# A two-layer graph attention kernel: row factors, attention columns and one transpose of the first two graphs on TensorE, their work interleaved

## The chip, the cores and the metric

The kernel runs on one core of a Trainium2 chip. The metric is the device time of the whole launch in microseconds (us). Engines are called PE (TensorE), DVE (VectorE), ACT (ScalarE), POOL (GpSimd) and SP (SyncE, which only issues DMAs here). PE has a clock that can be granted in full or in part; the profile calls it PEclk.

## What is computed

64 graphs of 256 nodes with 512 features in float32 go through two layers. Cut to what matters:

```python
# layer 0: 8 heads of 64 units
feats   = einsum('bnf,hfu->bhnu', X, W)
e_self  = einsum('bhnu,hu->bhn', feats, a_self)
e_neigh = einsum('bhnu,hu->bhn', feats, a_neigh)
dense   = leaky_relu(e_self[..., :, None] + e_neigh[..., None, :], 0.2)
att     = softmax(dense + -1e10 * (1 - A[:, None]), -1)
x = layernorm(x + relu(einsum('bhij,bhju->bhiu', att, feats) + b))
# layer 1: 8 heads of 64, q, k, v from W_qkv
attn = 0.33 * softmax(q k^T / 8) + 0.33 * adj + 0.33 * exp(-adj)
x = layernorm(x + (attn v) W_out + b_out)
```

`e_self` and `e_neigh` are linear in X, so the kernel computes them as two more columns per head of the weights of layer 0: W times a_self and W times a_neigh (the "attention columns", U and U + 1 of `wf`). The exponential of the leaky sum is split into a factor for each row (`grow`, for every head a row of 256 values and the maximum of the neighbour term), which all 128 partitions need, and a factor for each column (`ccol`); `pT` is the larger of row factor and column factor, times the mask `at`.

## The kernel before

A graph has 2 tiles (T) of 128 nodes and 4 blocks (C) of 128 features. Its work is cut into stages: `proj0` (features of layer 0), `attend0`, `proj1` (q, k and v), `softmax1` and `attend1`. Each stage is a set of steps, and a list written by hand gives their order: `start` for what comes before the loop, `attention0_beside_projections1(b)` and `attention1_beside_projections0(b)` for each graph, and `end`. `do(stage, graph, step)` emits a step, and `in_order` ties every engine to the order of the source. The loop is a pipeline over graphs: in pass b, layer 0's attention of graph b runs beside the q, k, v of graph b - 1, the softmax of b - 1, the output of b - 2 and the features of b + 1.

The products with wf, wqk and wv take seven products of half blocks in place of eight (`seven`, L281): they need sums of the left side (`xC`, `hC`, made by `left_factors`) and of the weights (`right_factors`, L220, and `combine`, L251). Products are named p1 to p7. "qk p1" is the first product of q and k of a graph, the rows `pq_p<-hT` of the profile.

What the change touches, for the first graphs:

- The attention columns. DVE multiplies each of 8 pieces of W with a_self and a_neigh, copied to every partition (`a_bc`), and adds up (L211, L216).
- The features of graph 0 (`features`, L469) use plain W and the transposed rows of x (`xT_rows`); those of graph 1 are seven products (`pf_p`).
- The row factors (`rows`, L419): four transposes (`pr`), a maximum, an exponential and a clamp of 8 rows; then `gs` goes to DRAM and comes back to all partitions as `gb` (1028 KB). `columns` (L441) needs the maximum out of it, `weights` (L517) the rows.
- The output of layer 0 of each graph (`X1`) goes to DRAM as rows (`hs`) and comes back in blocks of 32 (`hb`, L635); DVE transposes the blocks into `hT` (L639), the input of `proj1`.
- `norm0`, `end`, `squares` and `norm` are the layer norm of both tiles of a graph at once: sums on DVE, squares on ACT, three small steps on POOL (L350 to L354), the scaling on ACT (L358).
- The weights of layer 1 are loaded after `start`, and `combine` runs after the first list of graph 0.

PSUM has two pools: "mm" with 4 banks and "sc" with 2 buffers of two banks.

Of the kernel before, what the change touches and what calls it, by code (L numbers as in the profile page):

```python
# [8 lines left out]
FT = mybir.dt.float32  # L9
# [8 lines left out]
def kernel(  # L18
# [29 lines left out]
    nc = tc.nc  # L48
# [99 lines left out]
    a_bc = io.tile([P, 2, H, U], FT, tag="x1", name="a_bc", bufs=3)  # L148
    for k, a in enumerate((a_self, a_neigh)):
        nc.sync.dma_start(  # L150
            a_bc[:, k].rearrange("p h u -> p (h u)"),
            a.rearrange("h u -> (h u)").partition_broadcast(P),
        )
    for c in range(C):
        for g in range(2):
            nc.sync.dma_start(
                wf[c // C2][g][:, c % C2, :, :U],
                w0[g * HG : (g + 1) * HG, c * P : (c + 1) * P, :].rearrange("h p u -> p h u"),
            )
        if c == 1:  # L160
            load_rows(0)
# [45 lines left out]
    for c in range(C):  # L207
        for g in range(2):
            w = wf[c // C2][g][:, c % C2]
            prod = work.tile([P, 2, HG, U], FT, tag="pT", name=f"wa_{c}_{g}", bufs=4)  # L210
            nc.vector.tensor_mul(  # L211
                prod,
                w[:, :, :U].unsqueeze(1).to_broadcast([P, 2, HG, U]),
                a_bc[:, :, g * HG : (g + 1) * HG, :],
            )
            nc.vector.tensor_reduce(  # L216
                w[:, :, U:].rearrange("p h s -> p s h"), prod, AX.X, ALU.add
            )

# [8 lines left out]
    def load_weights1():  # L228

        wk1 = work.tile([P, C2, F], FT, tag="p", name="wk1", bufs=4)  # L230
        wv12 = work.tile([P, C2, F2], FT, tag="both", name="wv12", bufs=4)
        parts = w_qkv.rearrange("(k c p) (h s u) -> s k c p h u", k=2, p=P, s=3, u=U)

        def get(dst, s, k, heads=slice(0, H)):
            for c in range(C2):
                nc.sync.dma_start(
                    dst[:, c].rearrange("p (h u) -> p h u", u=U), parts[s, k, c][:, heads]
                )

        get(wqk_sb[:, 0], 0, 0)  # L240
        get(wqk_sb[:, 1], 0, 1)
        get(wk1, 1, 0)
        get(wqk_sb[:, 6], 1, 1)
        get(wv_sb[:, 0], 2, 0, slice(0, HG))
        get(wv12, 2, 0, slice(HG, H))
        get(wv_sb[:, 1], 2, 1, slice(0, HG))
        get(wv_sb[:, 2], 2, 1, slice(HG, H))
        nc.sync.dma_start(bo_bc, b_out.partition_broadcast(P))
        nc.sync.dma_start(wo_sb, w_out.rearrange("(c p) f -> p c f", p=P))

        def combine():  # L251
            q1, q2, s1, s2, s3, s4, k2 = (wqk_sb[:, i] for i in range(7))
            nc.vector.tensor_add(s1, wk1, k2)
            nc.vector.tensor_sub(s2, s1, q1)
            nc.vector.tensor_sub(s3, q1, wk1)
            nc.vector.tensor_sub(s4, q2, s2)
            right_factors(wv_sb, wv12)

        return combine
# [67 lines left out]
    class LayerNorm:  # L327
# [9 lines left out]
        def mean(self):  # L337
            nc.gpsimd.tensor_scalar_mul(self.nmean, self.sums, -1.0 / F)  # L338

        def squares(self):  # L340
            for t in range(T):
                junk = small.tile([P, F], BF, tag="junk", name="junk", bufs=1)
                nc.scalar.activation(  # L343
                    junk,
                    self.src[:, t, :],
                    AF.Square,
                    bias=self.nmean[:, t : t + 1],
                    accum_out=self.rstd[:, t : t + 1],
                )
            nc.gpsimd.tensor_scalar(  # L350
                self.rstd, self.rstd, 1.0 / F, EPS, op0=ALU.mult, op1=ALU.add
            )
            nc.gpsimd.tensor_tensor(self.rstd, self.rstd, mhalf, op=ALU.pow)
            nc.gpsimd.tensor_mul(self.shift, self.nmean, self.rstd)  # L354

        def apply(self):
            for t in range(T):
                nc.scalar.activation(  # L358
                    self.src[:, t, :],
                    self.src[:, t, :],  # L360
                    AF.Identity,
                    bias=self.shift[:, t : t + 1],
                    scale=self.rstd[:, t : t + 1],
                )


    V0, GB, CCOL, AT, CT = {}, {}, {}, {}, {}

    def proj0(b):
        xT = work.tile([P, C, N], FT, tag="xT", name=f"xT_{b}")  # L370
        xC = work.tile([P, 4, C2, P], FT, tag="xC", name=f"xC_{b}", bufs=1)

        V0[b] = work.tile([P, T, H, UX], FT, tag="v0", name=f"v0_{b}", bufs=1)
        GB[b] = work.tile([P, H, N + 1], FT, tag="gb", name=f"gb_{b}", bufs=1)
# [44 lines left out]
        def rows():  # L419
            pr = ps_tile([H, 2, N], f"pr_{b}")  # L420
            for s in range(2):
# [15 lines left out]
                GB[b].rearrange("p h n -> p (h n)"),  # L437
                gs.rearrange("h n -> (h n)").partition_broadcast(P),
            )

        def columns():  # L441
            nd = small.tile([P, T, H], FT, tag="nd", name=f"nd_{b}", bufs=2)
            nc.vector.tensor_sub(
                nd,
                V0[b][:, :, :, U + 1],
                GB[b][:, :, N].unsqueeze(1).to_broadcast([P, T, H]),
            )
            nc.scalar.activation(CCOL[b], nd, AF.Exp, scale=0.8)  # L448
            nc.scalar.activation(V0[b][:, :, :, U], nd, AF.Exp, scale=0.2)

        def halves(t, g):
            return V0[b][:, t, g * HG : (g + 1) * HG]

        product, add = seven_rows(
            f"pf_{b}",
            xT,
            xC,
            wf_sb,
            [P, HG, UX],
            {10 * (t + 1) + g + 1: halves(t, g) for t in range(T) for g in range(2)},  # L460
        )
# [7 lines left out]
        def features(t):  # L469

            for g in range(2):
                pf = ps_tile([P, HG, UX], f"pf_{b}_{t}_{g}")
                for c in range(C):
                    matmul(
                        pf,
                        xT[:, c, t * P : (t + 1) * P],
                        wf[c // C2][g][:, c % C2],
                        start=(c == 0),
                        stop=(c == C - 1),
                    )  # L480
                nc.vector.tensor_add(halves(t, g), pf, b0_bc[:, g * HG : (g + 1) * HG])
# [10 lines left out]
        def transposes():  # L492
            transpose_blocks(xT, XB[b])
            left_factors(xC, xT)

        return dict(
            xT=transposes,
# [16 lines left out]
    def attend0(b):  # L514
        pT = {}

        def weights(h):  # L517
            pT[h] = work.tile([P, T, N], FT, tag="pT", name=f"pT_{b}_{h}", bufs=4)
            for j in range(T):
                nc.vector.scalar_tensor_tensor(  # L520
                    pT[h][:, j, :],
                    GB[b][:, h, :N],
# [37 lines left out]
        def end():  # L560
            ln = NORM["l0", b] = LayerNorm(X1[b], b, "l0")
            for t in range(T):
# [9 lines left out]
            ln.mean()  # L572
            X.pop(b)
# [6 lines left out]
            squares=lambda: NORM["l0", b].squares(),  # L580
            norm=lambda: NORM.pop(("l0", b)).apply(),
# [5 lines left out]
    def proj1(b):  # L587
# [4 lines left out]
        hb = io.tile([P, C, N // B, B], FT, tag="hb", name=f"hb_{b}", bufs=1)  # L592
        hs = dram.tile([N, F], FT, tag="hs", name=f"hs_{b}")
# [45 lines left out]
        def transposes():  # L639
            transpose_blocks(hT, hb)  # L640
            left_factors(hC, hT)

        return dict(
            blocks=rows_to_blocks,
# [220 lines left out]
    def start():  # L865
        do("proj0", 0, "xT_rows")
        for t in range(T):
            do("proj0", 0, "features", t)
        do("proj0", 0, "rows")
        do("proj0", 0, "aT")  # L870
        do("proj0", 0, "far")
        do("proj0", 0, "shared")
        do("proj0", 0, "columns")
        for h in range(H):
            do("proj0", 0, "scaled", h)

    def attention0_beside_projections1(b):


        do("attend1", b - 3, "squares")  # L880
        do("proj1", b - 1, "qk", "p1")
        do("proj1", b - 1, "qk", "p2")
        if b > 0:
            do("proj0", b, "columns")
        do("proj1", b - 1, "qk", "p6")
        for h in range(HG):
            if b > 0:
                do("proj0", b, "scaled", h)
            do("attend0", b, "weights", h)
        do("attend1", b - 3, "store")  # L890
        do("proj1", b - 1, "qk_add", 11)
        do("proj1", b - 1, "qk", "p5")
        do("proj1", b - 1, "qk", "p7")
        do("attend1", b - 2, "residual")
        do("proj1", b - 1, "qk_add", 22)
        do("attend0", b, "product", 0, 0)
        if b > 0:
            for h in range(HG, H):
                do("proj0", b, "scaled", h)
        do("proj1", b - 1, "qk", "p4")  # L900
# [6 lines left out]
        do("proj1", b - 1, "qk", "p3")  # L907
        do("proj1", b - 1, "qk_add", 12)
        do("proj0", b + 1, "xT")
        if b + 2 < NB:  # L910
            load(b + 2)
# [115 lines left out]
    in_order()  # L1027
    start()
    if NB > 1:
        load(1)  # L1030
        load_adj(1)
    right_factors(wf_sb, wf12)
    combine_weights1 = load_weights1()
    in_order()
    for b in range(NB):
        attention0_beside_projections1(b)
        if b == 0:
            combine_weights1()
            in_order()
# [50 lines left out]
```

The softmax here doesn't subtract the row's maximum and nothing guards it: scores larger than these inputs give would overflow.

## Time and profile before

| | |
|---|---|
| Median of 3 runs | 3186.19 us (3185.43 to 3191.53) |
| Span of the profiled run | 3185.4 us, mean clock of PE 0.990 |
| PE busy | 3116.4 us, 98% |
| DVE busy | 2647.0 us, 83% |
| ACT busy | 1485.6 us, 47% |
| The chain that ended last | PE 85%, DVE 8%, DMA 4% |
| qk p1 of graph 0, 1, 2, 3 starts | 74.57, 118.61, 169.76, 218.37 us |

How to read it: an engine row gives the time in which the engine worked, its share of the span and the number of its instructions. A busy PE isn't yet a PE at its peak, since its matmuls are pipelined. In the time lines a row gives the start, the length, the engine, the line of the source, the operation with output and inputs, the shape and the count, and in brackets the idle time before it with what ended it. Each float32 matmul of the source is two rows of the trace; a transpose is one.

### The profile page before, as it was taken

The numbers are of one execution on the slowest core, as the hardware profiler recorded it, in microseconds if no ns is written. First come the engines' busy times: TensorE is split into PE (matmuls) and PEld (weight loads), VectorE is DVE, ScalarE is ACT, GpSimd is POOL, SyncE is SP. The second block draws the span as 40 slices with busy tenths as digits, with TensorE's granted clock in tenths as the row PEclk, the third lists the DMA queues.
The fourth block names the chain that finished last, engine by engine and source line by source line (L and its number), as shares of the span: only waits on it lengthen the run. The fifth ranks groups of instructions, "written<-read, shape, count | busy, mean of one in ns | idle before, by whom it ended". The sixth has DMA issues, their size and how long they took to land.

```text
span 3185.4 us, 56122 instructions
## 1 busy us (share of the span) xinstructions
PE 3116.4 (98%) x21262; PEld 2502.0 (79%) x21262; DVE 2647.0 (83%) x5152; ACT 1485.6 (47%) x3585; POOL 176.2 (6%) x518
## 2 busy tenths in 40 slices
PE   5999999999999999999999999999999999999997
PEld 4887877877878878878878778778788788788784
DVE  6788888888888888888888888888888888888885
ACT  1444444454454454444444444544544544454442
POOL 0000000000000000000000000000000000000000
PEclk7999999999999999999999999999999999999998
DMA  7344344344343443443443443443443434434421
GB/s 157 76 113 108 98 114 97 102 121 94 104 115 93 112 106 97 111 106 98 114 104 100 115 95 104 121 94 104 121 94 104 115 94 109 105 99 112 108 81 53
DMA packets 764394, 331.88 MB, mean 104 GB/s; under 512 B 696672, under 2 KB 697440, under 8 KB 747744
## 3 DMA queue, kind: packets, MB, share of 16 engines
q1 hardware_dynamic: 764128, 328.30, 40.9%
q8 instruction: 171, 2.80, 0.4%
q14 instruction: 95, 0.78, 0.1%
HBM read 259.80 MB, written 68.16 MB: 103 GB/s over the span
## 4 chain that ended last, share of the span: by engine, by line
PE 85%; DVE 8%; DMA 4%; SPq 1%; issue 1%; ACT 1%; POOL 0%; ACTq 0%; DVEq 0%; POOLq 0%
PE pq_p L292 21%; PE po L828 13%; PE av L539 12%; PE pf_p L292 11%; PE pv_p L292 11%; PE pz L668 7%; PE av L767 7%; DVE pT L520 2%; PE pd L697 2%; DMA gb<-gs 2%; DVE p L757 1%; DVE p L750 1%; PE pr L82 1%; DMA rb<-rs 1%; DVE qk L304 0%
## 5 line engine op out<-in xcount | busy, mean ns | idle before, releaser
L539 PEld LDWEIGHTS av<-v,pT 128*128 128x128 f32 x4096 | 493.9, 194 | 19.0 <-ACT v L485 12.5
L539 PE MATMUL av<-v,pT 128*128 128x65 f32 x4096 | 491.7, 274 | 12.2 <-ACT v L485 12.2
L292 PE MATMUL pq_p<-hC,wqk_sb 128*128 128x128 f32 x4096 | 482.4, 276 | 2.6 <-ACT qk L301 2.6
L292 PEld LDWEIGHTS pq_p<-hC,wqk_sb 128*128 128x128 f32 x4096 | 467.8, 192 | 3.2 <-ACT qk L301 3.2
L828 PE MATMUL po<-wo_sb,oT 128*128 128x512 f32 x1008 | 459.5, 599 | 0.0
L520 DVE SCALAR_TENSOR_TENSOR pT<-gb,ccol,at 128x256 f32<-128x256 f32 x1024 | 416.9, 479 | 24.6 <-ACT ccol L448 17.8
L301 ACT COPY v<-pv_p 128x256 f32<-128x256 f32 x256 | 95.6, 373 | 669.9 <-PE pv_p L292 669.9
L292 PE MATMUL pq_p<-hT,wqk_sb 128*128 128x128 f32 x3072 | 376.0, 279 | 4.8 <-DVE hT L121 4.8
L292 PEld LDWEIGHTS pq_p<-hT,wqk_sb 128*128 128x128 f32 x3072 | 355.2, 193 | 31.3 <-DVE hC L270 24.3
L828 PEld LDWEIGHTS po<-wo_sb,oT 128*128 128x128 f32 x1008 | 181.6, 190 | 204.0 <-issue 202.7
L677 ACT ACTIVATE p<-pz,hide 128x512 f32<-128x512 f32 x512 | 310.3, 689 | 59.3 <-PE pz L668 59.3
L757 DVE TENSOR_TENSOR p<-p,ct 128x1024 f32<-128x1024 f32 x256 | 313.5, 1225 | 8.8
L750 DVE TENSOR_TENSOR p<-p,rb 128x1024 f32<-128x1024 f32 x256 | 309.2, 1208 | 9.2 <-DMA rb<-rs 9.0
L343 ACT ACTIVATE junk<-x,nmean_l 128x512 bf16<-128x512 f32 x256 | 185.0, 723 | 263.7 <-POOL nmean_l L338 259.5
L292 PE MATMUL pv_p<-wv_sb,hC 128*128 128x256 f32 x1024 | 260.5, 387 | 4.8 <-DVE v L304 4.5
L689 DVE SCALAR_TENSOR_TENSOR both<-p 128x512 f32<-128x512 f32 x256 | 176.6, 691 | 98.7 <-ACT p L677 98.5
L485 ACT ACTIVATE v<-v 128x64 f32<-128x64 f32 x1024 | 258.5, 339 | 0.0
L292 PE MATMUL pf_p<-wf_sb,xC 128*128 128x264 f32 x1008 | 256.7, 388 | 0.5 <-ACT v L301 0.5
L668 PE MATMUL pz<-qk 64*128 64x256 f32 x2048 | 256.2, 389 | 0.9 <-ACT p L677 0.8
L767 PE MATMUL av<-p,v 128*64 128x256 f32 x2016 | 245.6, 385 | 0.9 <-DVE p L757 0.9
L668 PEld LDWEIGHTS pz<-qk 64*128 64x128 f32 x2048 | 187.1, 186 | 67.9 <-ACT p L677 26.0
L292 PEld LDWEIGHTS pf_p<-wf_sb,xC 128*128 128x128 f32 x1008 | 191.9, 191 | 33.4 <-ACT v L301 1.3
(107 smaller groups left out, 3693.1 us busy)
## 6 DMA issues: line engine op xcount, KB each, us to landing
gb<-gs SPq DMA_DIRECT2D x64, 1028.0 KB
rb<-rs SPq DMA_DIRECT2D x64, 1024.0 KB, 4.7
x<-in_x_dram SPq DMA_DIRECT2D x64, 512.0 KB
hs<-x SPq DMA_DIRECT2D x64, 512.0 KB
hb<-hs SPq DMA_DIRECT2D x256, 128.0 KB, 3.5
out_dram<-x SPq DMA_DIRECT2D x64, 512.0 KB, 3.0
xb<-in_x_dram SPq DMA_DIRECT2D x252, 128.0 KB, 3.7
adj<-in_adj_dram SPq DMA_DIRECT2D x256, 64.0 KB, 4.5
```

Of the source, the lines that this page charges most:

```text
L292: matmul(d, lhsT, rhs, start=(p in FIRST and i == 0), stop=(i == len(todo) - 1), skip_group_check=True,)
L343: nc.scalar.activation(junk, self.src[:, t, :], AF.Square, bias=self.nmean[:, t : t + 1], accum_out=self.rstd[:, t : t + 1],)
L485: nc.scalar.activation(V0[b][:, t, h, :U], V0[b][:, t, h, :U], AF.Copy, scale=V0[b][:, t, h, U : U + 1],)
L520: nc.vector.scalar_tensor_tensor(pT[h][:, j, :], GB[b][:, h, :N], CCOL[b][:, j, h : h + 1], AT[b][:, j, :], op0=ALU.max, op1=ALU.mult,)
L539: matmul(av[:, k, :], pT[h][:, j, t * P : (t + 1) * P], V0[b][:, j, h, :UA], start=(j == 0), stop=(j == T - 1),)
L668: matmul(pz[:, r, j, :], QK[b][rows, g, 1, j * P : (j + 1) * P], QK[b][rows, g, 0, :], start=True, stop=True,)
L677: nc.scalar.activation(p[:, :, j, :], pz[:, :, j, :], AF.Exp, bias=hide[:, j, b : b + 1], scale=U**-0.5,)
L689: nc.vector.scalar_tensor_tensor(both[g], p[:, :, 0, :], TINY, p[:, :, 1, :], op0=ALU.add, op1=ALU.add)
L750: nc.vector.tensor_mul(p, p, REC[b][:, k : k + 2, g // 2, :] .unsqueeze(2) .to_broadcast([P, 2, T, N]),)
L757: nc.vector.tensor_add(p, p, CT[b].unsqueeze(1).to_broadcast([P, 2, T, N]))
L767: matmul(av[0][r * U : (r + 1) * U, g % 2, :], V1[b][:, j, 2 * g + r, :], PROBS[b][g][:, r, j, :], start=(j == 0), stop=(j == T - 1),)
L828: matmul(po, oT[:, c, t * P : (t + 1) * P], wo_sb[:, c, :], start=(c == 0), stop=(c == C - 1),)
```

## The change

The first two graphs (0 and 1) get an order and some steps of their own; from graph 2 on the steps are those of before. For graphs 0 and 1:

- The attention columns are made by PE: W's blocks are transposed by a product with the identity (`pw`, 64 columns for each head), copied by ACT (`wT`) and multiplied with `a2`, which holds a_self and a_neigh of a pair of heads as columns (`pwa`). DVE copies the few results into wf.
- The row factors stay on the chip: PE spreads each of the 8 rows over all partitions by a product with a selector of ones (`pg`), and DVE's `weights` reads them in PSUM; the maximum is spread by a product with a diagonal.
- Graph 1's features use plain weights too, so that wf's right factors can wait until graph 2.
- Graph 0's output is transposed by PE (`ph`) and not sent through DRAM; its layer norm runs by tiles.
- `start` holds all of graph 0's layer 0 and, between its steps, graph 1's features and row factors and graph 0's q and k; the loop starts with b = 1. The weights of layer 1 are loaded at the start, their combinations are spread over the list in four parts, and w0 is loaded by ACT's queue.

It is for keeping PE at work before the pipeline has filled. The core of the diff:

```diff
+    for g in range(2):
+        for c in range(C):
+            nc.scalar.dma_start(
...
+    a2 = consts.tile([P, HG, 2, 2], FT, name="a2")
+    nc.vector.memset(a2, 0.0)
+    for k, a in enumerate((a_self, a_neigh)):
+        for r in range(2):
+            nc.sync.dma_start(
+                a2[r * U : (r + 1) * U, :, r, k],
+                a.rearrange("(g r) u -> r u g", r=2)[r],
+            )
...
-            nc.vector.tensor_mul(
-                prod,
-                w[:, :, :U].unsqueeze(1).to_broadcast([P, 2, HG, U]),
-                a_bc[:, :, g * HG : (g + 1) * HG, :],
-            )
-            nc.vector.tensor_reduce(
-                w[:, :, U:].rearrange("p h s -> p s h"), prod, AX.X, ALU.add
-            )
...
+    def attention_vectors():
+
+        pwa = ps_tile([P, HG, C, 4], "pwa")
+        for g in range(HG):
+            pw = psum.tile([P, C, P], FT, tag="sc", name=f"pw_{g}", bufs=2)
+            for c in range(C):
+                for r in range(2):
+                    matmul(
+                        pw[r * U : (r + 1) * U, c, :],
+                        wf[c // C2][g // 2][:, c % C2, 2 * (g % 2) + r, :U],
+                        ident,
+                        start=True,
+                        stop=True,
+                    )
+            wT = work.tile([P, C, P], FT, tag="pT", name=f"wT_{g}", bufs=4)
+            nc.scalar.copy(wT, pw)
+            for c in range(C):
+                matmul(pwa[:, g, c, :], wT[:, c, :], a2[:, g], start=True, stop=True)
...
+        def maxima():
...
+            diag = small.tile([H, H], FT, tag="diag", name=f"diag_{b}", bufs=1)
+            nc.vector.tensor_scalar_mul(diag, ident[:H, :H], grow[:, N : N + 1])
+            matmul(pr[:, 1, :H], SEL[0][:, H, :], diag, start=True, stop=True)
...
+        def factors():
...
+            for g in range(2):
+                pg = psum.tile([P, HG, N], FT, tag="sc", name=f"pg_{b}_{g}", bufs=2)
+                for k in range(HG):
+                    matmul(
+                        pg[:, k, :],
+                        SEL[0][:, g * HG + k, :],
+                        grow[:, :N],
+                        start=True,
+                        stop=True,
+                    )
...
+        def from_rows(t):
...
+            for c in range(C):
+                transpose(PT[0][:, t, c, :], X1[b][:, t, c * P : (c + 1) * P])
+            nc.scalar.copy(hT[:, :, t * P : (t + 1) * P], PT[0][:, t])
...
     def start():
...
+        attention_vectors()
+        in_order()
+        for g in range(2):
+            for t in range(T):
+                do("proj0", 0, "features", t, g)
+                do("proj0", 0, "copied", t, g)
...
+        do("proj0", 0, "maxima")
+        do("proj0", 0, "columns")
+        do("proj0", 0, "factors")
+        do("proj0", 1, "xT")
...
+        do("attend0", 0, "end", tiles[0])
+        do("attend0", 0, "squares", tiles[0])
+        do("attend0", 0, "norm0", 0, 1)
+        do("attend0", 0, "norm0", 1, 1)
+        do("attend0", 0, "end", tiles[1])
+        do("attend0", 0, "squares", tiles[1])
+        do("attend0", 0, "norm", tiles[0])
+        do("proj1", 0, "from_rows", 0)
+        do("attend0", 0, "norm", tiles[1])
...
+        combine_weights1(0)
+        do("proj1", 0, "qk", "p1")
+        do("proj1", 0, "from_rows", 1)
+        do("proj1", 0, "hC")
+        do("proj1", 0, "qk", "p2")
+        do("proj1", 0, "qk", "p6")
+        do("proj1", 0, "qk_add", 11)
...
-    for b in range(NB):
+    for b in range(1, NB):
         attention0_beside_projections1(b)
```

What `start` leaves out above, in order: weights and scaling of heads 0 to 3, features of graph 1's first tile, products of these heads, the same for heads 4 to 7 and the second tile, `norm0` of the first tile; and after the add of q: copies of graph 1's second tile, `combine` 1, `shared` of graph 0, adjacency and `far` of graph 1, qk p5 and p7, `maxima`, `columns` and `factors` of graph 1, `combine` 2 and an add.

In the first pass of the loop (b = 1) the steps come in this order: weights of heads 0 to 3, qk p4 and p3, products, weights of heads 4 to 7, `norm0` of the first half, `shared` of graph 1, the right factors of wv and then of wf, xT of graph 2, the values of graph 0, and the features of graph 2.

## The prediction

> **What bounds the kernel now.** I read the page first, then the busy time in stretches, then the time lines of TensorE (PE), VectorE (DVE) and ScalarE (ACT) over the first 125 us.
>
> ```profile
> PE 3116.4 (98%) x21262; PEld 2502.0 (79%) x21262; DVE 2647.0 (83%) x5152; ACT 1485.6 (47%) x3585; POOL 176.2 (6%) x518
> ...
> PEclk7999999999999999999999999999999999999998
> ```
>
> ```profile
> 0.00:118.61 118.61, 76.33 (x426) 65.50 (x426) 74.84 (x161) 34.16 (x87) 3.33 (x14) 0.81 0.59 127
> 118.61:169.76 51.15, 48.77 (x332) 38.88 (x332) 41.74 (x83) 20.36 (x50) 1.82 (x4) 1.00 0.39 93
> 169.76:218.37 48.61, 48.51 (x336) 38.81 (x332) 41.01 (x81) 23.20 (x56) 2.88 (x8) 1.00 0.41 107
> ```
>
> The columns are stretch, length, busy time of PE, weight loads, DVE, ACT, POOL, then the clock. From 169.8 us on PE is never idle and a graph takes 48.6 us. The change touches nothing there: only what runs before qk p1 of graph 1, which starts at 118.61 us. So the question is when that point comes. Before it PE is idle for 42 us and its clock averages 0.81. The time line says where:
>
> ```profile
> 35.88 13.89 PE L539 MATMUL av<-v,pT 128*128 128x65 f32 x64 [12.21 <-ACT v L485]
> ...
> 70.86 1.01 PE L82 MATMUL pr<-ident,v 128*8 128x128 f32 x4 [11.51 <-DVE v L465]
> 74.57 6.07 PE L292 MATMUL pq_p<-hT,wqk_sb 128*128 128x128 f32 x32 [2.70 <-DVE hT L121]
> ...
> 118.61 3.84 PE L292 MATMUL pq_p<-hT,wqk_sb 128*128 128x128 f32 x32 [2.13 <-DVE hT L121]
> ...
> 127.71 2.05 PE L292 MATMUL pq_p<-hC,wqk_sb 128*128 128x128 f32 x16 [1.69 <-ACT qk L301]
> ```
>
> ```profile
> 32.56 0.18 DVE L443 TENSOR_TENSOR nd<-v,gb 128x16 f32<-128x16 f32 x1 [3.35 <-DMA gb<-gs]
> ...
> 81.80 3.26 DVE L520 SCALAR_TENSOR_TENSOR pT<-gb,ccol,at 128x256 f32<-128x256 f32 x8 [0.28 <-ACT ccol L448]
> ```
>
> ```profile
> 107.04 1.52 ACT L358 ACTIVATE x<-x,shift_l,rstd_l 128x512 f32<-128x512 f32 x2 [0.30 <-POOL shift_l L354]
> ```
>
> A line is start, length, engine, line and tiles, and in brackets the idle time before it and what ended it. The reader sees three holes of PE (12.2, 11.5 and 2.7 us), the round trip of the row factors through DRAM in front of the first, and the chain of graph 1: weights pT at 81.80, norm done at 107.04 + 1.52 = 108.56, then rows to DRAM and back, hT, and 118.61.
>
> The clock needs its own look, in stretches of 3.41 us:
>
> ```profile
> 48.57:51.98 3.41, 3.07 (x10) 2.11 (x9) 2.10 (x7) 0.25 (x1) 0.00 (x0) 0.50 0.84 191
> 51.98:55.39 3.41, 3.23 (x7) 2.53 (x8) 0.24 (x2) 1.19 (x4) 0.22 (x1) 0.50 0.68 168
> 55.39:58.81 3.42, 3.42 (x17) 2.92 (x16) 1.49 (x3) 2.39 (x6) 1.10 (x3) 1.00 0.82 297
> 58.81:62.22 3.41, 0.54 (x3) 0.12 (x1) 2.80 (x4) 2.05 (x5) 0.00 (x0) 1.00 0.98 164
> ```
>
> The 64 av of the 35.88 line ran without a pause for 14 us and stayed at half clock (0.50 in every stretch to 51.98); the 264-wide pf_p filled one stretch and the next ran at 1.00; a stretch with 0.54 us of work lost it again.
>
> **What the Trainium skill says.** "TensorE: Matmul & The Clock Gate", Part 1, "What's actually happening": half rate by default, full rate after a busy window of about 3.4 us, windows that run freely. The trace agrees (changes near 28.1, 55.4, 62.2 and 79.3 us, whole windows apart) and adds that narrow work doesn't count as busy: an av takes 217 ns at half clock for 65 columns, a 128-wide pq_p 230. Same page, "LDWEIGHTS (loading the stationary operand)": the load goes by columns. The trace has 190 ns for 128 columns, 137 for 64. Same page, Part 3, "The mechanism": tiles in different places of the array run together. The trace agrees: 16 av of layer 1, 64 columns to each half, take 1.88 us (117 ns each), where full-width pv_p of the same 256 take 216. "DMA: Bandwidth & Descriptors", "Rules for kernel authors": a last dimension that isn't contiguous costs a descriptor per element. That concerns a2 (1024 floats); no run here shows it.
>
> **The change, part by part**, on the clock of the run. Steps come from the rows named; a hand-over between engines costs 0.05 to 0.2 us in the trace.
>
> *Start.* Rows of x come first now, w0 on ACT's queue. Before, 16 KB, 1 MB and x had landed at 10.18. About 1 MB is ahead of the second half of x and the first four w0 blocks: with 0.2 MB by 4 us and 0.77 by 6 us (98 and 283 GB/s), some 7 us. ACT's table load (1.28) now stands behind its eight DMA issues, and the seventh waits for a2. So the first wT copy is done near 11.2 (10.4 to 12.5).
>
> *Attention columns on PE.* Removed: eight pairs of DVE operations (1.32 us each, 7.2 to 17.8). Added: four groups, strictly one after another in PE's order. A group is 8 source matmuls, 16 instructions, to 64 columns (16 x 125 ns = 2.0 us at half clock, 1.0 at full), a wait for ACT's copy (0.16 + 0.59 + 0.06 = 0.81), and 8 instructions against a2, bound by weight loads like av (8 x 217 = 1.74, or 8 x 108 = 0.87). That is 4.55 us at half clock, 2.7 at full. Dense share: 2.0 of 4.55, 44%, less than the av that never woke the clock. I take half clock: 11.2 + 1.74 + 3 x 4.55 = 26.6 us.
>
> *Features of graph 0.* 32 instructions: about 5.1 us at half clock until a full window has passed (11.5 at 445 ns), the rest at 222 ns: 9.7 us, to 36.3. Before: 22.6. This part loses 13.7 us.
>
> *Row factors.* Removed: clamp, gs and gb (25.2 to 32.5) and the right factors of wf ahead of pT (2.6 us). Now: copy 0.45, four transposes 0.6, reduce 0.41, nb 0.14, exp 0.47, the diagonal product, which by the built order waits for exp (0.25), nd 0.18, clamp 0.28, with hand-overs to 39.55; then 8 pg of 216 ns (1.73) and pT, whose first instruction waits for the whole pg tile: 41.4. Before: 35.26. Half of the loss is regained.
>
> *Both graphs.* PE from 39.55: 16 pg 3.5, 32 features of graph 1 7.1, 64 av at full clock 6.9: to 57.1 without a hole; scaled (16 x 246 ns) and pT (2 x 3.3) are hidden beside it. Before, av and pf_p of graph 1 ended at 59.35.
>
> *Norm and hT of graph 0.* Removed: hs and hb by DRAM, DVE's hT, and the queue of combinations on DVE (59.7 to 69.5) before them. Now the last av ends at 55.3 and everything is a chain: norm0 0.65, end 0.75, mean 0.25, squares 0.95, three POOL steps 1.2, the second mean behind them, second squares 0.9, since ACT holds both squares ahead of the first norm, norm 0.8, four transposes 0.5, copy 0.65: qk p1 at 62.5 (before 74.57). PE is idle from 57.1 to 61.25, so its clock falls: p1 3.7 us, and hT's second half is copied only behind it, at 67.9.
>
> *DVE from there.* It sat idle for it; then hC 1.55, add 0.69 (p2 ends 69.3), two copies 0.86, s3 1.22, shared 2.6, adjacency 0.7: 75.6. ACT's far and at (1.6) and copy (0.6) stand before exp (0.5), then diagonal, nd, clamp, pg: 81.1; pT of graph 1 at 81.2. Before: 81.80. The 12 us won at p1 are gone again.
>
> *Graph 1 to the junction.* pT 3.3 and 3.3 with 2.8 for the wait on p3 and its add, norm0 1.2, shared 2.65, and then what was done earlier before: right factors of wv and wf, 2 x 2.75. PE waits for wv's: values p6 at 95.9. xT and xC of graph 2 2.8, add 0.45, norm0 1.2, end 1.45: 105.8. Mean, squares, POOL, norm as before (102.57 to 108.56, less 1.0 of waiting): 110.8. Before: 108.56.
>
> Sum: the junction comes 110.8 - 108.56 = 2.2 us later, at 120.8; gb of graph 2, which made the 1.69 us wait at 127.71, stands behind the same hs, hb and adjacency issues, so it moves alike. 3186.2 + 2.2 = 3188.4. DMA isn't in it: wqk and wv (3 MB, at the 220 GB/s of 40 to 48 us) land by 36 us, needed at 59; wo_sb now goes out near 76 beside nothing urgent.
>
> **Rivals.**
> 1. *The clock wakes in the attention columns*, or the gaps are shorter than ACT's row says. For it: the 16 transposing matmuls use both halves of the array. Against: the 48.57 stretch held 1 us of av (half streaming) and 1.8 us of pf_p, two thirds of 3.41 in all, and didn't wake it. Three and a half groups save 1.85 us each, features 2.5, p1 2.4: 11.4 less, 3177.
> 2. *More half clock and more waits.* PE is nearly idle from 36.3 to 39.55 and 75 to 79.3; a fall costs 2.6 and 2.0. Pairs that don't overlap cost 4 x 1.5 more, and a2's small descriptors 1 to 3. Half of that, 6 to 9: 3196.
> 3. *All waits hide; PE alone counts.* Added at full clock: 4 + 3.5 for the columns, 6.9 pg, 1.4 transposes, 0.9 for plain features: 16.7 on some 60.6 of before, 77, plus 8 at the start: 85, 33 us won, 3153. Against: the in-order waits above.
>
> **How the numbers follow.** Forecast (no change that can be told) 0.53, rival 1 0.18, rival 3 0.04, rival 2 0.25. Errors of some 5 us pile up over eight stages, so the range goes past rivals 1 and 2: 3176 to 3200. Faster is rivals 1 and 3, 0.22; slower is rival 2, 0.25.
>
> **What would show it.** Right: clock at 0.5 until the features of graph 0, these done near 36 us; PE idle for 4 us before the transposes ph; qk p1 of graph 0 near 62, pT of graph 1 near 81, norm of graph 1 done near 111, graph 1's qk p1 near 121, 48.6 us a graph after it. Wrong: a full clock in the pw rows, features done before 30, or DVE not idle ahead of hC. If the time per graph after 170 us differs, the whole frame is wrong.

## The result, and the profile after

The changed kernel takes 3205.61 us (median of 4 runs, 3200.9 to 3207.67) where the kernel before takes 3187.68 in the same comparison: the ratio is 1.0053, interval 1.0035 to 1.0070. It is 18 us slower. The forecast of 3188.4 and its range up to 3200 are both too low. The profiled execution has a span of 3205.9 us, 20.5 more than before.

From the page, engine totals and the clock's row:

```profile
PE 3150.4 (98%) x21406; PEld 2529.3 (79%) x21406; DVE 2634.2 (82%) x5144; ACT 1487.0 (46%) x3587; POOL 178.4 (6%) x522
...
PEclk9899999999999999999999999999999999999999
```

PE has 34 us more busy time for 144 more rows, and the clock's second slice, from 80 to 160 us, is now below 9. The first slice reads 9 where it read 7 before, but that is no gain: the time ahead of the first change of the clock in a trace (30.96 us here, 14.43 before) is counted as full clock, here and in the clock column of every stretch that takes in the start, while the rows there show half clock (eight pwa in 1.87 us, against 1.05 at full clock in e12; six pf of the kernel before in 2.92 us, 487 ns each against 222). The page shows no more than that; the first 135 us have to be cut into stretches. The three stretches that answer to those of before, bounded by qk p1 of graphs 1, 2 and 3 (columns as there: PE, weight loads, DVE, ACT and POOL busy, then the clock):

```profile
0.00:134.20 134.20, 107.49 (x571) 90.50 (x571) 62.53 (x153) 36.07 (x89) 5.71 (x18) 0.86 0.43 85
134.20:186.26 52.06, 50.13 (x333) 40.59 (x333) 41.87 (x83) 20.25 (x50) 1.33 (x4) 0.97 0.38 93
186.26:234.50 48.24, 48.24 (x337) 38.89 (x333) 41.00 (x81) 23.19 (x56) 2.63 (x8) 1.00 0.40 106
```

The pipeline from there is as fast as before (48.24 against 48.61 us). The junction, qk p1 of graph 1, comes at 134.20 in place of 118.61: 15.6 of the 20.5 us. The next stretch loses 0.9 more, with a short fall of the clock in it (0.97), and the one behind it gives 0.4 back. The rest, 4.4 us, lies in single passes of the loop that take 49 to 50 us among passes of 48.24; both kernels have them, at different places. I take them for scatter: from qk p1 of graph 3 to the end, where all kernels of this text have the same steps, their fourteen traces take 2965.5 to 2971.5 us (2967.0 before, 2971.4 after the change). In front of the junction PE is busy for 107.5 us, not 76.3, and still 27 us idle. The time line of PE says with what:

```profile
39.22 5.29 PE L501 MATMUL pg<-grow,sel 8*128 8x256 f32 x16 [0.46 <-DVE grow L494]
...
65.81 1.12 PE L82 MATMUL ph<-ident,x 128*128 128x128 f32 x4 [5.08 <-ACT x L353]
67.60 3.78 PE L286 MATMUL pq_p<-hT,wqk_sb 128*128 128x128 f32 x16 [0.68 <-ACT hT L739]
...
83.36 7.19 PE L501 MATMUL pg<-grow,sel 8*128 8x256 f32 x16 [0.46 <-DVE grow L494]
90.48 3.78 PE L286 MATMUL pq_p<-hC,wqk_sb 128*128 128x128 f32 x16
94.05 2.80 PE L286 MATMUL pq_p<-hT,wqk_sb 128*128 128x128 f32 x16
...
107.31 3.75 PE L286 MATMUL pv_p<-wv_sb,hC 128*128 128x256 f32 x8 [2.90 <-DVE wv_sb L215]
...
134.20 3.84 PE L286 MATMUL pq_p<-hT,wqk_sb 128*128 128x128 f32 x32 [2.45 <-DVE hT L121]
```

Read the lengths against each other. A set of sixteen rows of pq_p takes 1.95 us at full clock (at 71.98 in this trace); here the first (behind ph) takes 3.78 and the two behind pg 3.78 and 2.80. The sixteen rows of pg take 5.29 and 7.19 us, where the forecast had 3.46. In stretches of 3.41 us from one clock change to the next, over the second pg and what follows it:

```profile
82.16:85.58 3.42, 2.81 (x7) 2.32 (x8) 2.10 (x4) 2.45 (x11) 0.00 (x0) 0.50 0.51 61
85.58:88.99 3.41, 3.41 (x9) 2.66 (x8) 1.75 (x5) 0.00 (x0) 0.00 (x0) 0.50 0.62 117
88.99:92.40 3.41, 3.41 (x13) 2.59 (x12) 1.48 (x4) 0.00 (x0) 0.00 (x0) 0.50 0.71 266
92.40:95.82 3.42, 3.42 (x18) 3.42 (x18) 0.00 (x0) 1.52 (x6) 0.00 (x0) 0.50 0.00 1
95.82:99.23 3.41, 3.41 (x33) 3.41 (x32) 0.85 (x2) 0.97 (x5) 0.00 (x0) 1.00 0.00 0
```

PE is busy for the whole of 85.58 to 88.99, all of it pg, and the clock stays at half. It comes back only after a stretch that holds nothing but pq_p (92.40 to 95.82). The time line of DVE shows the other two things that come late:

```profile
72.80 0.42 DVE L262 TENSOR_TENSOR hC<-hT 128x256 f32<-128x256 f32 x1 [7.56 <-ACT hT L739]
...
87.24 3.23 DVE L604 SCALAR_TENSOR_TENSOR pT<-pg,ccol,at 128x256 f32<-128x256 f32 x8 [2.21 <-PE pg L501]
...
106.47 0.69 DVE L215 TENSOR_TENSOR wv_sb<-wv_sb 128x512 f32<-128x512 f32 x1
```

DVE does nothing for 7.56 us ahead of hC, and then PE waits 2.90 us at 107.31 for one of DVE's combinations of wv, work that needs nothing but weights.

Two stretches of the same trace end where the clock falls a third and a fourth time, ahead of the second pg and ahead of values p6 (pv_p at 107.31):

```profile
78.75:82.17 3.42, 1.11 (x11) 0.75 (x9) 1.78 (x5) 2.30 (x5) 0.00 (x0) 1.00 0.19 33
...
102.65:106.06 3.41, 1.76 (x16) 1.62 (x15) 3.31 (x9) 0.00 (x0) 0.00 (x0) 1.00 0.00 0
```

PE works for 1.11 and 1.76 us in them.

### The profile page after: what moved, and what is told of

It reads as the page before. It is cut to its first block, busy times and chain, and to the rows that moved or that the text cites. A ratio compares the mean times of both kernels' runs of the same rounds, so it can differ in the third digit from the quotient of the medians.

```text
span 3205.9 us, 56356 instructions
## 1 busy us (share of the span) xinstructions
PE 3150.4 (98%) x21406; PEld 2529.3 (79%) x21406; DVE 2634.2 (82%) x5144; ACT 1487.0 (46%) x3587; POOL 178.4 (6%) x522
## 3 DMA queue, kind: packets, MB, share of 16 engines
q10 hardware_dynamic: 4224, 1.05, 0.2%
## 4 chain that ended last, share of the span: by engine, by line
PE 87%; DVE 7%; DMA 3%; ACT 1%; issue 1%; POOL 0%; SPq 0%; ACTq 0%; POOLq 0%; DVEq 0%
PE pq_p L286 21%; PE po L928 13%; PE av L623 12%; PE pf_p L286 11%; PE pv_p L286 11%; PE pz L768 7%; PE av L867 7%; DMA gb<-gs 2%; DVE pT L604 2%; PE pd L797 2%; PE pr L82 1%; DVE p L857 1%; DVE p L850 1%; DVE qk L298 1%; PE pf L548 1%
## 5 line engine op out<-in xcount | busy, mean ns | idle before, releaser
L604 DVE SCALAR_TENSOR_TENSOR pT<-gb,ccol,at 128x256 f32<-128x256 f32 x992 | 403.6, 479 | 20.1 <-ACT ccol L519 17.6
L768 PEld LDWEIGHTS pz<-qk 64*128 64x128 f32 x2048 | 187.1, 186 | 67.9 <-ACT p L777 26.0
```

The costliest lines, as they stand in the source:

```text
L604: nc.vector.scalar_tensor_tensor(pT[h][:, j, :], GB[b][h], CCOL[b][:, j, h : h + 1], AT[b][:, j, :], op0=ALU.max, op1=ALU.mult,)
L768: matmul(pz[:, r, j, :], QK[b][rows, g, 1, j * P : (j + 1) * P], QK[b][rows, g, 0, :], start=True, stop=True,)
```

## The experiments

Theory A: the loss is clock; the 8-row pg of the row factors don't count as work and let the clock fall. Theory B: it is the waits of the new order. Theory C: it is the attention columns on PE, 14 us to the end of graph 0's features. Theory D: it is DVE's work moved behind hC. "On 8 rows" means that a product uses 8 of the 128 rows of PE's array (8 partitions of both operands); "sixteen rows" of a product are rows of the trace. In the table "junction" is qk p1 of graph 1 in the one execution that was profiled, whose own time stands beside it, and ratios are to the kernel before, measured beside each set.

| Kernel | Median us | Ratio, interval | Profiled us | Junction |
|---|---|---|---|---|
| changed kernel | 3205.61 | 1.0053, 1.0035 to 1.0070 | 3207.67 | 134.20 |
| e1, pg on 128 rows | 3197.41 | 1.0025, 1.0015 to 1.0036 | 3200.75 | 126.68 |
| e2, e1 and unread products | 3187.99 | 0.9992, 0.9983 to 1.0000 | 3187.38 | 119.74 |
| e3, columns on DVE | 3192.49 | 1.0008, 1.0000 to 1.0017 | 3189.7 | 119.28 |
| e4, DVE's work early | 3194.79 | 1.0016, 1.0009 to 1.0024 | 3198.32 | 125.06 |
| e5, all four | 3172.53 | 0.9948, 0.9935 to 0.9960 | 3171.55 | 103.40 |
| e6, e5 without unread products | 3174.33 | 0.9956, 0.9944 to 0.9969 | 3174.33 | 103.87 |
| e7, unread products alone | 3194.56 | 1.0016, 1.0009 to 1.0023 | 3197.54 | 127.22 |
| e8, before with unread products | 3187.84 | 0.9998, 0.9990 to 1.0007 | 3187.33 | 120.40 |
| e9, e6 with pg on 8 rows | 3185.19 | 0.9986, 0.9980 to 0.9993 | 3182.41 | 114.35 |
| e10, columns in paired order | 3197.28 | 1.0024, 1.0015 to 1.0032 | 3202.78 | 129.74 |
| e11, pg on 32 rows | 3202.61 | 1.0037, 1.0025 to 1.0050 | 3203.3 | 133.78 |
| e12, e10, e1 and e4 | 3182.17 | 0.9976, 0.9967 to 0.9984 | 3178.69 | 108.97 |

The changed kernel has four runs, from the first set, in which the kernel before was some 2 us faster than in the later ones (3187.68 against 3189.2 to 3189.7). So a difference in us from the changed kernel is good to a few us only: the interval of its ratio alone spans 11.

### e1: pg on all 128 rows

```diff
-        sel = SEL[0] = work.tile([H, H + 1, P], FT, tag="rb", name="sel", bufs=1)
+        sel = SEL[0] = work.tile([P, H + 1, P], FT, tag="rb", name="sel", bufs=1)
+        nc.vector.memset(sel, 0.0)
...
-            grow = small.tile([H, N + 1], FT, tag="grow", name=f"grow_{b}", bufs=1)
+            full = small.tile([P, N + 1], FT, tag="grow", name=f"grow_{b}", bufs=1)
+            nc.gpsimd.memset(full, 0.0)
+            grow = full[:H]
```

The pg products read `full` and all of `sel`; the added rows are zeros, so the result and the number of PE's instructions are the same.

> The changed kernel with the selector and the row factors padded with zeros from 8 to 128 partitions: pg has the same count and the same 256 columns, but all 128 rows of the array are loaded. Same result. Theory A (PE's clock fell and stayed low because products of 8 rows don't count as busy): pg of graph 1 goes from 450 to about 216 ns after at most one window, qk p4 and p3 run at full clock, qk p1 of graph 1 comes 4 to 8 us earlier, about 3200 us. Theory B (the time went into waits of the new order and into attention columns finished 14 us later): pg is as slow as before or its gain is swallowed, no more than 1.5 us, about 3205.

Measured: 3197.41, 8.2 us less than the changed kernel, junction at 126.68. The first pg take 3.69 us and the clock doesn't fall in them. The second start at half clock, since it fell in front of them. The stretches of e1 from 78.40 on, in which the pg lie from 79.08 to 85.81:

```profile
78.40:81.81 3.41, 2.86 (x9) 2.25 (x9) 2.10 (x4) 2.36 (x10) 0.00 (x0) 0.50 0.49 63
81.81:85.23 3.42, 3.42 (x10) 2.70 (x9) 2.29 (x6) 0.00 (x0) 0.00 (x0) 0.50 0.91 232
85.23:88.64 3.41, 3.41 (x30) 3.36 (x29) 0.93 (x3) 1.01 (x4) 0.00 (x0) 1.00 0.37 145
```

The second line is the twin of the changed kernel's second line above: nothing but pg, PE busy throughout, at half clock, with one row more. But behind it the clock is at 1.00. Zeros in 120 more rows wake the clock where the same instructions on 8 rows don't. That is what theory A said, and some 8 of the 18 us.

### e11: pg on 32 rows

As e1, with 32 in place of `P` for both tiles.

> Selector and row factors padded to 32 rows in place of 128. If the clock goes by the share of the array's rows that a product uses: 32 of 128 count as a quarter, pg(1) stays at half clock through p4 and p3 as in the changed kernel, time 3203 to 3207. If it only takes some least number of rows: as with 128, time 3196 to 3199, clock back at 85 us.

Measured: 3202.61, junction 133.78. The times alone don't settle it, since the interval of its ratio overlaps that of the changed kernel and that of e1; the trace does. The second pg of e11:

```profile
83.13 7.16 PE L505 MATMUL pg<-grow,sel 32*128 32x256 f32 x16 [0.56 <-DVE grow L498]
90.22 3.78 PE L286 MATMUL pq_p<-hC,wqk_sb 128*128 128x128 f32 x16
93.79 2.88 PE L286 MATMUL pq_p<-hT,wqk_sb 128*128 128x128 f32 x16
```

This is the changed kernel's picture again, with e1's additional memsets in it, so these weren't what woke the clock in e1. A quarter of the rows isn't enough; where between 32 and 128 the line runs wasn't tried.

### e2 and e7: unread products in the holes

```diff
+    def fill(n, dst=None):
+        for _ in range(n):
+            matmul(
+                FILL[0] if dst is None else dst,
+                ident,
+                wqk_sb[:, 0, 0, :],
+                start=True,
+                stop=True,
+            )
+        in_order()
```

The calls are one behind the maxima of graph 0, four ahead of ph, two behind the maxima of graph 1 and three ahead of values p6. Their results are not read. e2 has them together with the full rows, e7 alone.

> The kernel of e1_full_rows with dense products that nobody reads (identity times a piece of wqk, 512 columns) in PE's gaps: one behind the transposes of graph 0's maxima, four ahead of ph, two behind the maxima of graph 1, three ahead of values p6. Same result. Theory A: the clock stays at full from the first features on, the qk p1 rows of graph 0 take 1.9 instead of 3.8 us, qk p1 of graph 1 comes 11 to 16 us earlier than in the changed kernel, about 3192 us. Theory B: PE only works more; not more than 2 us from e1_full_rows.

> The changed kernel with the unread products alone; pg stays on 8 rows. Theory A with my reading that 8-row products count as idle: the clock falls within the 16 pg of either graph in spite of the filling (3.5 us of pg hold at least one window that is mostly pg), pg x16 of graph 1 takes over 5 us, junction 123 to 130, time 3193 to 3200, several us above the 3188 of rows and filling together. If what matters is only that PE has something to do, rows or not: pg x16 takes 3.7 us, the clock holds, and the time is 3188 like that run's.

Measured: e2 3187.99 with the junction at 119.74, e7 3194.56 with 127.22. The same stretch of time, 31 to 119.78 us, in the changed kernel and then in e2:

```profile
31.00:119.78 88.78, 74.82 (x384) 64.81 (x384) 48.30 (x112) 21.55 (x63) 3.91 (x9) 0.79 0.29 54
```

```profile
31.04:119.78 88.74, 78.27 (x477) 62.66 (x476) 58.85 (x133) 31.57 (x82) 5.25 (x13) 1.00 0.37 76
```

In e2 the clock, up at 31.04, is never lost before the junction, and PE does 93 more instructions in 3.5 us more of busy time. Adding work that nobody reads takes 9.4 us off e1. So theory B alone falls: the order of the other steps is unchanged, and the loss is gone. e7 shows that filling the holes isn't enough: in its second pg (5.36 us) the clock still falls, at 83.2, and rows on top of filling are worth 6.6 us (3194.56 - 3187.99).

### e3: the attention columns back on DVE

```diff
     def attention_vectors():
-        pwa = ps_tile([P, HG, C, 4], "pwa")
...
+        for g in range(2):
+            for c in range(C):
...
+                nc.vector.tensor_mul(
...
+                nc.vector.tensor_reduce(
```

> The changed kernel with the attention columns undone: DVE multiplies and adds as in the kernel before, group by group, nothing of pw and pwa is left. Theory C (the attention columns on PE cost the chain 14 us and the rest of the start hands that on): features of graph 0 end near 23 instead of 36.4 us, everything after them 10 to 14 us earlier, about 3193 us. Against it: if later waits swallow what comes early (DMA, DVE), 0 to 3 us, 3203 or more.

Measured: 3192.49, 13.1 us less. The features of graph 0 end near 22.9 us, as before the change, and the junction is at 119.28. The clock is lost four times before that all the same, and both pg are slow (5.82 and 7.19 us). So theory C holds for its 13 us, and the 8-row pg have no part in them. It is the price that the forecast put on the columns (13.7 us to the end of these features). Part of it is half clock in the columns themselves: e12, below, has them at full clock for a while.

### e4: DVE's work ahead of hC

```diff
         combine_weights1(0)
+        do("proj0", 0, "shared")
+        combine_weights1(3)
+        right_factors(wf_sb, wf12)
+        in_order()
         do("proj1", 0, "qk", "p1")
```

The same lines are taken out of their later places.

> The changed kernel with graph 0's shared part and the right factors of wv and wf moved up into the 7.6 us in which DVE waits for hT, ahead of hC. Same result, same work. Theory D (work of DVE moved late in graph 1's chain): the 2.9 us wait of values p6 is gone, the norm of graph 1 comes 7 to 10 us earlier, about 3197 us. Theory A alone: only the clock fall behind that wait goes, 2 to 4 us, about 3202.

Measured: 3194.79, 10.8 us less. On DVE's time line of e4 the combinations of wv and wf now end where hC begins:

```profile
72.75 0.70 DVE L217 TENSOR_TENSOR wf_sb<-wf_sb 128x528 f32<-128x528 f32 x1
73.51 0.42 DVE L262 TENSOR_TENSOR hC<-hT 128x256 f32<-128x256 f32 x1
```

hC comes 0.7 us later than in the changed kernel, for 7.7 us of work placed ahead of it (65.78 to 73.45). Values p6 no longer waits, and the fall of the clock in that wait is gone as well. Theory D holds, but not for the wait alone: of the 9.1 us at the junction 4.3 lie behind the start of values p6 (107.31 to 134.20 in the changed kernel, 102.49 to 125.06 in e4), where products of the changed kernel ran at half clock.

### e5, e6 and e9: together

e6 is e1, e3 and e4 in one kernel; e5 has the unread products too (none ahead of values p6); e9 is e6 with pg on 8 rows.

> All four edits together: selector and row factors padded to 128 rows, unread products behind both maxima and before the transposes ph (none before values p6), attention columns on DVE, shared and two right factors moved ahead of hC. Theory A (the clock is the loss, and the late DVE work and the columns come on top): clock 1.0 from about 14 us to the junction, features of graph 0 done near 23 us, qk p1 of graph 1 at 106 to 112 us, time 3174 to 3182, faster than both kernels. Theory B (the waits of the new order are the loss, and the separate gains are the same gain counted several times): qk p1 of graph 1 stays at 117 to 120, time 3186 to 3190. If DVE, which now has the 10.5 us of the columns again, is the limit: in between, about 113.

> The same without the unread products. Theory A: the holes before ph and behind the maxima still lose the clock, each fall costing 3 to 5 us: junction at 112 to 117, time 3180 to 3186, and the difference from the run with the unread products is the price of the falls that remain. Theory B: no difference between the two, both near the time before.

> Attention columns on DVE and shared and right factors early, but pg on 8 rows and no unread products. Theory A with the reading that 8-row products count as idle: the clock falls at or behind pg of both graphs as in the changed kernel; junction 3 to 8 us behind the 103.9 of the run that also had full rows, 107 to 112, time 3177 to 3184. If the rows gain nothing once the rest is in order (hC waits for DVE anyway): 3174 to 3176.

Measured: e5 3172.53, e6 3174.33, e9 3185.19. The single gains of e1, e3 and e4 are 8.2, 13.1 and 10.8, together 32.1, which from 3205.6 gives 3173.5; e6 measured 3174.3. By the ratios to the kernel before it is 35 against 31 us. So the three parts add up as far as the runs can tell, and they weren't one loss of some 13 us seen three times. e5 and e6 both beat the kernel before, by 0.5 and 0.4%, and so the changed kernel by 1%; both lie below what I expected of them. Between those two the intervals overlap, and the junctions are 0.5 us apart: with the rest in order the falls that remain in e6 cost nothing that shows, since DVE, with the early work ahead of hC, starts hC only at 57.59 us in e6 and at 56.42 in e5. I expected 3 to 5 us for each; that was a miss. The full rows, however, are worth at least as much here as alone: 10.9 us from e9 to e6, 9.6 by the ratios, where e1 has 8.2 and 8.9. Second pg and what follows, of e9 and then of e6:

```profile
72.09 6.25 PE L490 MATMUL pg<-grow,sel 8*128 8x256 f32 x16 [0.46 <-DVE grow L483]
78.27 3.78 PE L284 MATMUL pq_p<-hC,wqk_sb 128*128 128x128 f32 x16
81.84 2.67 PE L284 MATMUL pq_p<-hT,wqk_sb 128*128 128x128 f32 x16
```

```profile
66.91 3.69 PE L494 MATMUL pg<-grow,sel 128*128 128x256 f32 x16 [0.55 <-DVE grow L487]
70.44 1.95 PE L284 MATMUL pq_p<-hC,wqk_sb 128*128 128x128 f32 x16
72.23 1.95 PE L284 MATMUL pq_p<-hT,wqk_sb 128*128 128x128 f32 x16
```

From the start of pg to the end of the three groups it takes 12.42 us in e9 (72.09 to 84.51) and 7.27 in e6 (66.91 to 74.18), with the same instructions in the same order.

### e8: the kernel before with unread products

24 products of 128x264 stand behind the row factors of graph 0 and 22 behind the features of graph 1, in its two long holes.

> The kernel before with 24 and 22 unread products of 128x264 in its two long holes of PE (12.2 us behind the transposes of the row factors of graph 0, 11.5 us behind the features of graph 1); nothing else is changed. Theory A (the clock was also what the kernel before lost at its start): clock 1.0 from 14.4 us on, the 64 av take 7 us and not 13.9, features of graph 1 end near 50 and not 59.35; what of this reaches qk p1 of graph 1 depends on DVE's combinations from 59.7 to 69.5, which follow the features: junction at 108 to 114, time 3177 to 3183. Theory B (chains of DVE and DMA set the start, PE's clock doesn't): junction within 2 us of 118.6, time within 0.1% of before.

Measured: 3187.84, no difference that can be told. But the edit didn't do what it was for: the clock was not kept. PE's time line and then the stretches of e8:

```profile
25.12 10.85 PE L868 MATMUL fill<-wf_sb,ident 128*128 128x264 f32 x48
37.41 13.24 PE L539 MATMUL av<-v,pT 128*128 128x65 f32 x64 [1.45 <-ACT v L485]
```

```profile
37.25:40.66 3.41, 3.25 (x19) 2.59 (x19) 2.79 (x8) 1.35 (x6) 0.00 (x0) 1.00 0.51 85
40.66:44.07 3.41, 3.41 (x19) 3.41 (x18) 2.76 (x7) 0.00 (x0) 0.00 (x0) 0.50 0.99 216
```

The av start at full clock, show 3.25 us of busy PE in a stretch, and lose it. The busy time overstates their work: most come two rows at a time, every 0.4 us, each pair behind a pT of DVE; 19 rows fall in the stretch. Where av come without such waits they keep the clock. In e1 a group of 32 fills one stretch, with the edges of two pf, and the clock is still full in the next one:

```profile
51.09:54.50 3.41, 3.41 (x34) 3.41 (x32) 0.00 (x0) 0.00 (x0) 0.00 (x0) 1.00 0.00 0
54.50:57.91 3.41, 1.98 (x10) 1.37 (x9) 3.05 (x11) 0.81 (x2) 0.83 (x2) 1.00 0.00 0
```

Whether the start of the kernel before would gain from a full clock stays open.

### e10 and e12: the columns on PE, better ordered

In e10 pwa of a group comes behind pw of the next, so PE has no wait for ACT's copy between groups.

```diff
             nc.scalar.copy(wT, pw)
-            for c in range(C):
-                matmul(pwa[:, g, c, :], wT[:, c, :], a2[:, g], start=True, stop=True)
...
+            turned.append(wT)
+            if g > 0:
+                pair(g - 1)
+        pair(HG - 1)
```

e12 is that with e1 and e4.

> The changed kernel; the products pwa of a group come behind the transposing products pw of the next, so PE doesn't wait for ACT's copies (0.69 us a group, 1.87 in the first). Waits alone: features of graph 0 end 2.5 to 4 us earlier, 32.5 to 34, still at half clock (0.5) until 24 us, junction 130 to 132, time 3201 to 3204. My first rival (the waits keep the clock from waking): clock 1.0 from about 14 us, features done near 27, junction 125, time 3196.

> Attention columns on PE in the paired order, full rows and the early DVE work together, no unread products. If the gains add up (about 3 us for the pairs, 7 for the rows, 9 to 11 for the early work from a junction at 134.2): junction 113 to 116, time 3182 to 3186, a little faster than before but slower than with the columns on DVE (3174). If the pairs wake the clock: 3176 to 3180.

Measured: e10 3197.28, 8.3 us less than the changed kernel, where I expected 2 to 5 for the waits alone; e12 3182.17. The trace of e10 is of the slowest of its fourteen executions (3202.78), with a junction 4.5 us earlier, which is what the waits alone would give; why the others are shorter no trace shows. In the profiled execution of e10 the clock was up from 9.6 to 13.0 us, in that of e12 from 12.2 to 19.1 us, so features of graph 0 ended at 31.9 and 27.3 us, in place of 36.1. e12 has these products at full clock:

```profile
12.87 0.66 PE L385 MATMUL pw<-ident,wf 128*64 128x128 f32 x8
13.35 0.61 PE L385 MATMUL pw<-ident,wf_sb 128*64 128x128 f32 x8
13.89 1.05 PE L372 MATMUL pwa<-a,wT 128*128 128x4 f32 x8
```

My first rival is thus possible with pw in longer rows, but not steady: PE has the same products for the columns in both kernels, and only e12's trace has them at full clock for longer than one window of 3.41 us. The spread of the runs doesn't decide it: twelve runs of e12 spread over 10 us (3178.16 to 3188.14), but 41 of the kernel before over 12.4. And in their best order the columns on PE remain behind e6, by 7.8 us in the medians.

## Why the prediction was wrong

Step by step, with the forecast first and the measurement second:

- *Start and attention columns*: PE reaches the features at 26.6; measured 26.60. Features of graph 0 end at 36.3; measured 36.1. Half clock in the pw, the gaps (0.69 us for 0.81) and the end came as worked out; the first copy was 0.3 us late and the four groups made up for it. Right.
- *Row factors, graph 0*: first pT at 41.4; measured 41.33. Right, because the pg that pT waits for ran before the clock fell at 41.2.
- *Both graphs*: PE free at 57.1; measured 60.7. **This is the step that failed first**: "16 pg 3.5" took 5.29, and the features behind it 3.81 in place of 1.94 for the first eight rows.
- *Norm and hT*: qk p1 at 62.5, hC at 67.9; measured 67.60 and 72.80. The 5.1 us are the 3.6 from above and 1.5 of a slightly longer chain. The idle of DVE (7.56 us) was foreseen; that it held work which later stands on the path was seen too ("what was done earlier before"), and e4 confirms it.
- *DVE from there*: pT of graph 1 at 81.2; measured 87.24, of which 4.9 us come with hC. Step "8 pg of 216 ns (1.73)": at half clock they take 450 ns each.
- *Graph 1 to the junction*: xT of graph 2 at 100, measured 110.89; the junction at 120.8, measured 134.20. Here p4 and p3 came cold behind pg, and values p6 behind its wait for wv ("PE waits for wv's" was right) cold again, with the clock down from 106.1 to 116.3.

The junction was missed by 13.4 us. The step that failed is the price of pg: sixteen rows, twice, at 216 ns each, with a clock that they themselves were taken to keep. Measured were 331 and 450 ns, and behind the second other products ran at half clock for 5.3 us more (90.48 to 95.82). e1 puts 8 us on it alone, e6 against e9 11. The second step that failed is what the waits do to the clock. The fall ahead of ph was seen, and p1 priced at 3.7 us; those ahead of the second pg and of values p6 were put at nothing. e2 against e1 gives 9.4 for the holes. With both mended, in e2, the junction comes at 119.74, near the 120.8 of the forecast; that is a little luck, since the forecast had p1 at half clock and e2 has not.

The prediction came near the fact. It wrote that the trace "adds that narrow work doesn't count as busy", for av of 65 columns that didn't win the clock, and then priced pg, 256 columns but 8 rows, as if it counted. Its mean clock of 0.81 ahead of the junction was misread: with half clock up to 14.43 us it is about 0.75 (an estimate from the changes of the clock in the trace), and about 0.74 after the change. The second rival had the direction ("More half clock and more waits"), but not the cause: of its terms the falls came, while the pairs of pw overlapped as forecast (16 in 1.98 us) and a2 held up nothing. Its sum is wrong, too: its terms give 11.6 to 13.6 us and half of them 5.8 to 6.8, not "6 to 9"; even the whole, 3200 to 3202, stays below the 3205.61. That the columns on PE lose 13.7 us was right to 0.6 us (e3), and that the gain at p1 of graph 0 is spent before pT of graph 1 was right too.

The Trainium skill, "TensorE: Matmul & The Clock Gate", section "HAM oscillation — how this bites in real kernels", gives the rule as no idle gaps of PE above about 3.4 us. The runs here agree for ph: a gap of 5.08 us costs the clock. But they show that shorter gaps cost it too, with little work beside them: 2.44 us ahead of the second pg and 2.90 ahead of values p6. And a stretch without any gap fails to win the clock when the products use few rows (pg, 85.58 to 88.99) or few columns (av of the kernel before, up to 48.57), though such av can keep it (e1). Part 1, "What's actually happening", of the same page says that the windows run freely, so that the number of cold products changes from run to run; the 9 to 11 us between runs of e9, e10 and e12 would fit that, but the runs of the kernel before spread as far, and of each kernel only one execution has a trace, so it isn't shown.

## What to carry to other kernels

A product that spreads or selects a few rows can be padded with zeros to the full height of the array: it costs no instruction of TensorE, and here it was worth 8 to 11 us of clock. Before work is put behind a wait of another engine, look for what that engine could do in the wait with data that is already there (here 7.7 us of work, 5.2 of them weight combinations, for a hole of 7.56). Moving work from VectorE to TensorE at a kernel's start, where both are partly idle, is priced at the clock that TensorE has there, and with the whole chain in front of the next product (here 13 us).

## What the runs showed of the hardware that was not expected

- TensorE's clock doesn't go by PE being busy alone. A window of 3.41 us filled with nothing but 256-wide products at half clock leaves the clock at 0.50 where they use 8 rows (changed kernel, 85.58 to 88.99; e9, 73.09 to 76.51) or 32 (e11, 85.49 to 88.91). Behind it the clock is at 1.00 where they use 128, of which 120 are zeros (e1, 81.81 to 85.23; e12, 70.25 to 73.66).
- Zeros count: the added rows of e1 hold nothing but zeros in both operands.
- Products of 65 columns keep a full clock but don't win one back: 32 of them fill a window of e1 (51.09 to 54.50) and the clock stays at 1.00, while three windows of them at half clock in the kernel before (38.33 to 48.57) leave it at 0.50. In e8, where only 19 come in a window, a full clock is lost.
- Gaps of 2.44 and 2.90 us were enough to lose the clock, where PE worked for no more than 1.11 and 1.76 us of the window.
